# Two products on 64 partitions each for the image's row sums, and a spectrum kept in tiles of 128 partitions

## The chip, the cores and the metric

The kernel runs on one core of one Trainium2 chip. The metric is device time in microseconds (us) from launch to end; the number compared is the median of several executions.

## What is computed

A batch of 32 images of 56 x 56 pixels with 96 channels goes through two layers. Only the skeleton is kept here; `ln` is a normalization over the 96 channels.

```python
# layer 0: convolution
xz = einsum('bhwc,cd->bhwd', ln(x), w_in) + b_in        # 96 -> 2 * 192, first 192 kept
x  = x + silu(conv3x3(x1, conv_w) + conv_b)             # 192 -> 96
# layer 1: attention-like mixing by a Fourier transform over the 3136 tokens
h  = relu(bn1(einsum('bnc,hc->bnh', ln(t), w1)))        # 96 -> 192
X  = fft(h, axis=1, norm='ortho')
xr = relu(X.real * rd - X.imag * idg + rb)
xi = relu(X.imag * rd + X.real * idg + ib)
y  = ifft(xr + 1j * xi, axis=1, norm='ortho').real
t  = t + bn2(einsum('bnh,ch->bnc', y, w2))
# then a feed-forward layer 96 -> 384 -> 96 in 8-bit floats
t  = t + qlinear(relu(qlinear(ln(t), W1, b1)), W2, b2)
```

## The kernel before, in words

The work is a software pipeline over images. The class `Image` holds the state of one image, and `plan(b)` (L490) lists its steps: each `put(when, f, ...)` gives a step a due time in units of an eighth of an image. All steps of all images are sorted by due time (L556) and issued in that order. A scheduler of the language then places the instructions of each engine from that list; the order on TensorE is what it decides, and TensorE runs its products in that order. Pools with few buffers tie steps together: a step that takes a buffer waits until the buffer's earlier user has been read.

An image's 3136 tokens lie as 112 partitions times 28 columns, so that partition `2 * row + half` holds half of an image row. The steps that the change touches, with their lines:

- `fetch` (L335) loads columns of an image as `xl`; `take_in` (L343) computes their statistics with `stats` (L120) and scales them into `xa`.
- `image` (L144) multiplies `xa` with the constant `rows6_sb`, which forms the row sums that a fast convolution needs. One product of one column has 112 partitions of input, 97 columns of weights and 168 columns of output: 84 sums for each half of a row. The result `im` goes through ScalarE into `img`. Three columns share a PSUM tile of the pool `psq`, which has two buffers under the tag `q`; `conv` (L151, tiles `cv`) and `to_tokens` (L188, tiles `st`) use the same two.
- The Fourier transform has two stages with a trip through DRAM between them (`da`). The first is `product_a` (L200, tiles `ph`) and `transform_a` (L210, tiles `pa`). The second works on seven groups `g` of four frequency pairs each. `fetch_a` (L401) loads a group as `at`: 112 partitions, 4 pairs, 192 hidden channels. `forward` (L216, tiles `px`) multiplies one half `i` of the channels, 96 of them, of each pair with `fb_sb`; so the spectrum lies in tiles of 96 partitions, two for a group. Each tile then takes three ScalarE activations (L226 to L228), `parts` (L231: three VectorE operations and one of ScalarE) and `relus` (L243: two VectorE operations), which leave it in `gt`.
- `product_w2` (L248, tiles `pg`) multiplies by the output weights: for each pair two products of 96 partitions are added up. `inverse` (L259, tiles `pe`) transforms back, `store_back` (L429) stores the group to DRAM (`de`). When all seven groups are there, `fetch_y` (L432) reads `y`, and `back` (L438, `transform_out` L268, tiles `py`) does the last product.
- The feed-forward layer is `ffn_in` (L280, tiles `pf`) and `ffn_out` (L295, tiles `po`) in 8-bit floats.

All products but the last two are of 32-bit floats. Such a product runs as two passes, each a weight load and a matmul in the profile, so the profile counts two where the code has one; transposes (tiles `tp`, `st`) take one.

Due times of the second stage, which the change rewrites:

```python
for g in range(NS):
    put(max(FIRST + 7.4, g - 2.4), fetch_a, g)
    ...
    put(g + 1.15, second_w2, g)
    put(g + 1.35, second_back, g)
    put(g + 1.55, store_back, g)
```

Of the kernel before, what the change touches and what calls it, by code (L numbers as in the profile page):

```python
# [38 lines left out]
F32 = mybir.dt.float32  # L39
# [13 lines left out]
NS = NP // PG  # L53
H = 192
# [9 lines left out]
LN_W, LN_B, CONV_B, B_IN, BN1, BN2, RD, RB, NPAR = 0, 1, 2, 3, 5, 13, 17, 21, 25  # L64


def width(p):

    return 2 * N2 + (p < PG)


def first(p):

    return 2 * (2 * N2 * p + min(p, PG))
# [3 lines left out]
def hybrid_kernel(ctx: ExitStack, tc: tile.TileContext, x, par, w_in, conv_w, w1, w2, fw1, fb1, fw2, fb2, fa, fb, ib, ia, rows6, out):  # L78
# [8 lines left out]
    mhalf = const.tile([N1, N2], F32, name="mhalf")  # L87
# [7 lines left out]
    par_sb = const.tile([C, NPAR], F32, name="par_sb")  # L95
    convb = par_sb[:, CONV_B : CONV_B + 1]

    wv = const.tile([C + 1, WC, 3, C], F32, name="wv")
    rows6_sb = const.tile([N1, 2 * WC * WG], F32, name="rows6_sb")
    w1a = const.tile([C + 1, H], F32, name="w1a")  # L100
    w2a = const.tile([C, 2, C], F32, name="w2a")
# [6 lines left out]
    xas = [const.tile([N1, 8, C + 1], F32, name=f"xa{i}") for i in range(2)]  # L108
    img = const.tile([C + 1, 2, N2 + 2, WC, WG], F32, name="img")
    ys = [const.tile([113, G4, C], F32, name=f"y{i}") for i in range(4)]  # L110
    scal = const.tile([C, 3, 2], F32, name="scal")
# [8 lines left out]
    def stats(t, kind, b, i):  # L120


        n = t.shape[1]
        name = f"{kind}_{b}_{i}"
        st = stp.tile([N1, n, 3], F32, tag=f"st{kind}", name=f"st_{name}")
        for j in range(0, n, 2):
            nc.vector.bn_stats(  # L127
                st[:, j : j + 2].rearrange("p j s -> p (j s)"), t[:, j : j + 2, :C].rearrange("p j c -> p c j")
            )
        var = stp.tile([N1, n], F32, tag="var", name=f"var_{name}")  # L130
        nc.vector.tensor_scalar(var, st[:, :, 2], 1.0 / C, EPS, ALU.mult, ALU.add)  # L131
        rs = sums.tile([N1, n], F32, tag=f"rs{kind}", name=f"rs_{name}")
        nc.gpsimd.tensor_tensor(rs, var, mhalf[:, :n], ALU.pow)  # L133
        return st[:, :, 1], var, rs
# [9 lines left out]
    def image(xa, n, b, j0):  # L144

        ps = psq.tile([C + 1, n, 2, WC * WG], F32, tag="q", name=f"im_{b}_{j0}")
        for j in range(n):
            nc.tensor.matmul(ps[:, j], xa[:, j, :], rows6_sb, start=True, stop=True)  # L148
        nc.scalar.copy(img[:, :, j0 + 1 : j0 + 1 + n].rearrange("c h j k g -> c j h (k g)"), ps)
# [66 lines left out]
    def forward(at, b, g, i):  # L216

        w = width(g * PG)
        px = psum2.tile([C, PG, 2, w], F32, tag="c", name=f"px_{b}_{g}_{i}")
        for j in range(PG):  # L220
            p = g * PG + j
            nc.tensor.matmul(px[:, j], at[:, j, i * C : (i + 1) * C], fb_sb[:, first(p) : first(p + 1)], start=True, stop=True)  # L222
        idg, ibi = par_sb[:, RD + 2 + i : RD + 3 + i], par_sb[:, RB + 2 + i : RB + 3 + i]
        re, im = px[:, :, 0, :], px[:, :, 1, :]
        av = work.tile([C, 3, PG, w], F32, tag="av", name=f"av_{b}_{g}_{i}")
        nc.scalar.activation(av[:, 0], im, AF.Abs, scale=idg)  # L226
        nc.scalar.activation(av[:, 2], re, AF.Identity, scale=idg, bias=ibi)
        nc.scalar.activation(av[:, 1], re, AF.Relu, scale=scal[:, 0, i : i + 1], bias=scal[:, 1, i : i + 1])  # L228
        return px, av

    def parts(px, av, b, g, i):  # L231

        w = width(g * PG)
        rd, mrd = par_sb[:, RD + i : RD + i + 1], scal[:, 2, i : i + 1]
        re, im = px[:, :, 0, :], px[:, :, 1, :]
        sv = work.tile([C, 3, PG, w], F32, tag="sv", name=f"sv_{b}_{g}_{i}")
        nc.vector.scalar_tensor_tensor(sv[:, 0], re, rd, av[:, 0], ALU.mult, ALU.add)  # L237
        nc.vector.scalar_tensor_tensor(sv[:, 1], im, mrd, av[:, 2], ALU.mult, ALU.add)
        nc.scalar.activation(sv[:, 1], sv[:, 1], AF.Relu)
        nc.vector.scalar_tensor_tensor(sv[:, 2], im, rd, av[:, 2], ALU.mult, ALU.add)  # L240
        return sv

    def relus(sv, av, gt, i):  # L243
        rb = par_sb[:, RB + i : RB + i + 1]
        nc.vector.scalar_tensor_tensor(gt[:, i, :, 0, :], sv[:, 0], rb, av[:, 1], ALU.add, ALU.max)
        nc.vector.scalar_tensor_tensor(gt[:, i, :, 1, :], sv[:, 2], 0.0, sv[:, 1], ALU.max, ALU.subtract)  # L246

    def product_w2(gt, b, g):  # L248
        k = 2 * width(g * PG)
        pg = psum2.tile([k, PG, C], F32, tag="b", name=f"pg_{b}_{g}")  # L250
        for j in range(PG):
            for i in range(2):
                lhs = gt[:, i, j].rearrange("c r k -> c (r k)")
                nc.tensor.matmul(pg[:, j, :], lhs, w2a[:, i, :], start=(i == 0), stop=(i == 1))  # L254
        gw = work.tile([k, PG, C], F32, tag="gw", name=f"gw_{b}_{g}")
        nc.scalar.copy(gw, pg)
        return gw

    def inverse(gw, b, g):  # L259

        pe = psum2.tile([112, PG, C], F32, tag="b", name=f"pe_{b}_{g}")
        for j in range(PG):
            nc.tensor.matmul(pe[:, j, :], ib_sb[: gw.shape[0], g * PG + j, :], gw[:, j, :], start=True, stop=True)
        es = work.tile([112, PG, C], F32, tag="es", name=f"es_{b}_{g}")
        nc.scalar.copy(es, pe)
        return es
# [68 lines left out]
    def fetch(im, i):  # L335
# [4 lines left out]
        im.xl[i] = xnp.tile([N1, j1 - j0, C], F32, tag=tag, bufs=bufs, name=f"xl_{im.b}_{i}")  # L340
        nc.sync.dma_start(im.xl[i], im.tokens[:, j0:j1, :])

    def take_in(im, i):  # L343
# [5 lines left out]
        nc.vector.tensor_tensor(im.xa[i][:, :n, :C], xl, rs.unsqueeze(2).to_broadcast([N1, n, C]), ALU.mult)  # L349
# [57 lines left out]
    def second(im, g, i):  # L407
        im.held["px", g, i] = forward(im.at[g], im.b, g, i)
        if i == 1:
            im.at.pop(g)  # L410

    def second_parts(im, g, i):
        px, av = im.held.pop(("px", g, i))
        im.held["sv", g, i] = parts(px, av, im.b, g, i), av

    def second_relus(im, g, i):
        if i == 0:
            im.gt[g] = work.tile([C, 2, PG, 2, width(g * PG)], F32, tag="gt", name=f"gt_{im.b}_{g}")
        relus(*im.held.pop(("sv", g, i)), im.gt[g], i)

    def second_w2(im, g):
        im.gw[g] = product_w2(im.gt.pop(g), im.b, g)

    def second_back(im, g):
        if g == 0:
            im.de = dram.tile([NP, 112, C], F32, tag="de", name=f"de_{im.b}")
        im.held["es", g] = inverse(im.gw.pop(g), im.b, g)

    def store_back(im, g):  # L429
        nc.sync.dma_start(im.de[g * PG : (g + 1) * PG].rearrange("p m c -> m p c"), im.held.pop(("es", g)))  # L430
# [44 lines left out]
    def ffn_end(im, g):  # L475
        o = im.held["o", g] = w3.tile([N1, G4, C], F32, tag="o", name=f"o_{im.b}_{g}")
# [13 lines left out]
    def plan(b):  # L490
# [5 lines left out]
        for i, (j0, j1) in enumerate(LN_CHUNKS):  # L496
# [3 lines left out]
            ats = (-0.95, -0.7) if last else (0.2, 0.5, 0.85) if i == 2 else (0.25, 1.0, 1.5)  # L500
            put(at + ats[0] - (2.5 if b else 12), fetch, i)
            put(at + ats[0] - 1.15, take_in, i)
            for part, j in enumerate(range(0, j1 - j0, 3)):
                put(at + ats[part], make_image, i, j, min(3, j1 - j0 - j))
# [34 lines left out]
        for g in range(NS):  # L539
            put(max(FIRST + 7.4, g - 2.4), fetch_a, g)  # L540
            for i in range(2):
                at = g + 0.55 * i
                put(at, second, g, i)
                put(at + 0.22, second_parts, g, i)
                put(at + 0.42, second_relus, g, i)
            put(g + 1.15, second_w2, g)
            put(g + 1.35, second_back, g)
            put(g + 1.55, store_back, g)
# [21 lines left out]
    with tc.tile_pool(name="setup", bufs=1) as sp, tc.tile_pool(  # L570
# [3 lines left out]
        nc.sync.dma_start(par_sb, par)  # L574
        win = sp.tile([C, H], F32, name="win")
# [63 lines left out]
        w2s = sp.tile([C, H], F32, name="w2s")  # L639
        nc.sync.dma_start(w2s, w2)  # L640
        nc.vector.tensor_scalar(w2s, w2s, s2, None, ALU.mult)
        for g in range(2):
            ps = spp.tile([128, 512], F32, tag="ps", name=f"ps_w2{g}")
            nc.tensor.transpose(ps[:C, :C], w2s[:, g * C : (g + 1) * C], ident[:C, :C])
            nc.vector.tensor_copy(w2a[:, g, :], ps[:C, :C])
# [9 lines left out]
        nc.vector.tensor_scalar(scal[:, 0, :], par_sb[:, RD : RD + 2], 2.0, None, ALU.mult)  # L655
        nc.vector.tensor_scalar(scal[:, 1, :], par_sb[:, RB : RB + 2], 2.0, None, ALU.mult)
        nc.vector.tensor_scalar(scal[:, 2, :], par_sb[:, RD : RD + 2], -1.0, None, ALU.mult)
# [40 lines left out]
def dft_tables():  # L698
# [57 lines left out]
    rows6 = np.zeros((HW, 2, 2, WC, WG))  # L756
    for g in range(WG):
        for i in range(6):
            r = 4 * g + i - 1
            if 0 <= r < HW:  # L760
                for h in range(2):
                    rows6[r, h, h, :, g] = sums[:, i]
    tables = fa.reshape(N1, 112), fb.reshape(112, -1), ib.reshape(114, NP, 112), ia, rows6.reshape(N1, -1)
    return [np.ascontiguousarray(a, np.float32) for a in tables]

# [45 lines left out]
```

## Time and profile before

| what | value |
|---|---|
| median of 3 runs | 3287.43 us (3282.76 to 3293.95) |
| profiled execution, its own time | 3285.59 us |
| its span, first to last instruction | 3283.7 us |
| granted TensorE clock over the span | 0.989 |
| VectorE (DVE) busy | 2711.9 us, 83% |
| ScalarE (ACT) busy | 2319.2 us, 71% |
| GpSimd (POOL) busy | 586.2 us, 18% |
| DMA | 355.61 MB, mean 108 GB/s |

Busy time is the union of an engine's instructions in time. In the lists of groups each row is a line, an engine, an operation, the tile written, the tiles read, the shapes, the count, then busy us and mean ns of one. For TensorE the shapes read: partitions x weight columns of the weights, then partitions x columns of the moving operand. PE is TensorE's matmul, PEld its weight load. Matmuls are pipelined: one begins before the one ahead has ended, so what a matmul costs is read from start to start and not from its duration.

### The profile page before, as it was taken

To read this page: it belongs to the slowest core of one execution; us is meant where nothing else is said; L and a number is where in the kernel's file an instruction comes from. 1 tells how busy PE (TensorE), PEld (TensorE's weight loads), DVE (VectorE), ACT (ScalarE), POOL (GpSimd) and SP (SyncE) were. 2 spreads that over 40 slices of the span, in tenths; PEclk is the share of its full clock that TensorE was granted. 3 is DMA by queue.
4 is the path that set the end of the run, shared out by engine and by line. 5 is a ranking of instruction groups with operands and counts; after the bars stand their busy time and mean duration, and the time that the engine had idled before them with its cause. 6 is when DMAs were issued, how large, how long until landed. Compare 5 with 4: busy or idle time off the path is not lost. (4 is left out here: it accounts for less than half of the span.)

```text
span 3283.7 us, 69648 instructions
## 1 busy us (share of the span) xinstructions
PE 3201.2 (97%) x24597; PEld 2821.3 (86%) x24597; DVE 2711.9 (83%) x8306; ACT 2319.2 (71%) x5616; POOL 586.2 (18%) x397
## 2 busy tenths in 40 slices
PE   6999999999999999999999999999999999999987
PEld 5888888888888888888888888888888888888875
DVE  5568888888888888888888888888888888887887
ACT  2567777777777777777777776777777777777676
POOL 2111112111112111112111112111112111111111
PEclk9999999999999999999999999999999999999997
DMA  4343344433344433344433344433344333443331
GB/s 109 102 110 104 96 114 121 118 105 108 92 121 123 118 102 106 98 119 121 117 106 100 104 121 117 118 97 103 107 121 123 106 108 94 116 121 104 98 108 55
DMA packets 330839, 355.61 MB, mean 108 GB/s; under 512 B 125577, under 2 KB 283673, under 8 KB 330265
## 3 DMA queue, kind: packets, MB, share of 16 engines
q1 hardware_dynamic: 328482, 348.99, 38.5%
q8 instruction: 195, 3.19, 0.4%
q10 hardware_dynamic: 2008, 2.17, 0.2%
q14 instruction: 154, 1.25, 0.1%
HBM read 196.92 MB, written 154.14 MB: 107 GB/s over the span
## 5 line engine op out<-in xcount | busy, mean ns | idle before, releaser
L159 PE MATMUL cv<-img,wv 97*96 97x224 f32 (+1 forms) x4608 | 863.8, 330 | 6.2 <-DVE wv L607 5.4
L159 PEld LDWEIGHTS cv<-img,wv 97*96 97x96 f32 x4608 | 675.1, 163 | 88.1 <-issue 7.1
L133 POOL TENSOR_TENSOR rs_c<-var_c,mhalf 112x8 f32<-112x8 f32 (+1 forms) x128 | 194.1, 1517 | 1900.5 <-DVE var_a L131 994.0
L222 PEld LDWEIGHTS px<-fb_sb,at 112*96 112x96 f32 x3584 | 399.7, 164 | 87.7 <-issue 30.6
L222 PE MATMUL px<-fb_sb,at 112*96 112x112 f32 (+1 forms) x3584 | 429.8, 261 | 20.6 <-DMA at<-da 17.4
L254 PEld LDWEIGHTS pg<-w2a,gt 96*112 96x112 f32 (+1 forms) x3584 | 394.2, 179 | 33.4 <-DVE gt L246 2.9
L254 PE MATMUL pg<-w2a,gt 96*112 96x96 f32 (+1 forms) x3584 | 403.9, 262 | 1.4 <-DVE gt L246 0.6
L226 ACT ACTIVATE av<-px,par_sb 96x224 f32<-96x224 f32 (+1 forms) x448 | 200.1, 447 | 267.8 <-PE px L222 263.4
L284 ACT CAST h<-pf 128x448 f16<-128x448 f32 x672 | 362.5, 539 | 25.2 <-PE pf L282 22.2
L204 PE MATMUL ph<-w1a,n2t 97*112 97x192 f32 x1792 | 369.0, 328 | 1.5 <-ACT n2t L197 1.2
L213 PE MATMUL pa<-h,fa_sb 112*112 112x384 f32 x896 | 366.3, 491 | 0.1
L207 ACT ACTIVATE h<-ph,rs_b 112x192 f32<-112x192 f32 x896 | 330.3, 426 | 29.3 <-PE ph L204 27.9
L148 PE MATMUL im<-rows_sb,xa 112*97 112x168 f32 x1792 | 324.0, 308 | 11.3 <-DVE xa L349 9.6
L133 POOL TENSOR_TENSOR rs_b<-var_b,mhalf 112x8 f32<-112x8 f32 (+1 forms) x128 | 191.7, 1498 | 748.1 <-DVE var_b L131 423.9
L204 PEld LDWEIGHTS ph<-w1a,n2t 97*112 97x112 f32 x1792 | 286.8, 177 | 39.5 <-ACT n2t L197 1.8
L292 DVE TENSOR_SCALAR h<-h,b1q 128x448 f16<-128x448 f16 x658 | 214.2, 326 | 112.0 <-ACT h L284 110.7
L459 DVE TENSOR_SCALAR xn<-t,st_c,rs_c 112x96 f32<-112x96 f32 x896 | 240.0, 320 | 75.4 <-POOL rs_c L133 75.3
L148 PEld LDWEIGHTS im<-rows_sb,xa 112*97 112x97 f32 x1792 | 263.9, 165 | 35.0 <-issue 10.3
L214 ACT COPY u<-pa 112x384 f32<-112x384 f32 x448 | 216.5, 483 | 101.3 <-PE pa L213 97.4
L293 DVE CAST hq<-h 128x448 fp8e5<-128x448 f16 x672 | 257.2, 383 | 12.7 <-ACT h L290 5.9
L237 DVE SCALAR_TENSOR_TENSOR sv<-px,par_sb,av 96x224 f32<-96x224 f32 (+1 forms) x448 | 197.4, 441 | 70.9 <-ACT av L228 66.1
L282 PE MATMUL pf<-n3t,w1q 96*128 96x448 fp8e5 x672 | 242.2, 360 | 8.8 <-ACT h L284 7.6
(110 smaller groups left out, 6022.9 us busy)
## 6 DMA issues: line engine op xcount, KB each, us to landing
da<-u SPq DMA_DIRECT2D x224, 336.0 KB, 3.2
at<-da SPq DMA_DIRECT2D x224, 336.0 KB, 3.8
de<-es SPq DMA_DIRECT2D x224, 168.0 KB, 2.3
y<-de SPq DMA_DIRECT2D x224, 168.0 KB, 2.8
out<-o SPq DMA_DIRECT2D x224, 168.0 KB, 2.2
xl<-in_x SPq DMA_DIRECT2D x96, 336.0 KB, 3.9
x<-in_x SPq DMA_DIRECT2D x96, 336.0 KB, 3.2
xl<-in_x SPq DMA_DIRECT2D x32, 168.0 KB, 2.3
```

Source lines behind the costliest of these rows:

```text
L133: nc.gpsimd.tensor_tensor(rs, var, mhalf[:, :n], ALU.pow)
L148: nc.tensor.matmul(ps[:, j], xa[:, j, :], rows6_sb, start=True, stop=True)
L159: nc.tensor.matmul(ps[:, at], wv[:, k, dx, :], cols, start=(dx == 0), stop=(dx == 2))
L204: nc.tensor.matmul(ph[:, j, :], n2t[:, 2 * j2 + j, :], w1a, start=True, stop=True)
L207: nc.scalar.activation(h[:, j], ph[:, j], AF.Relu, scale=rs[:, 2 * j2 + j : 2 * j2 + j + 1])
L213: nc.tensor.matmul(pa, fa_sb, h, start=True, stop=True)
L222: nc.tensor.matmul(px[:, j], at[:, j, i * C : (i + 1) * C], fb_sb[:, first(p) : first(p + 1)], start=True, stop=True)
L254: nc.tensor.matmul(pg[:, j, :], lhs, w2a[:, i, :], start=(i == 0), stop=(i == 1))
L282: nc.tensor.matmul(pf, w1q[:, k * 128 : (k + 1) * 128], n3t, start=True, stop=True)
L284: nc.scalar.copy(h1, pf)
L293: nc.vector.tensor_copy(hq[:, k, :], h2, saturate=False)
L459: nc.vector.tensor_scalar(xc[:, j], im.t[i][:, at, :C], mu[:, at : at + 1], rs[:, at : at + 1], ALU.subtract, ALU.mult)
```

## The change

The image's row sums. The host lays a second copy of the input, `xh`, in which the left halves of the 56 rows are on partitions 0 to 55 and the right halves on partitions 64 to 119; the rest is zeros. One column now takes two products, one for each block of 64 partitions, with 84 columns of output each, into two PSUM tiles at once. A step does 4 columns in place of 3, and its result goes through two ScalarE copies.

The spectrum. The seven groups become four units of 8, 8, 8 and 4 frequency pairs. In a unit of 8 there are three tiles of 128 partitions: two hold channels 0 to 127 of four pairs each, the third holds channels 128 to 191 of all eight, four pairs on partitions 0 to 63 and four on 64 to 127. The third is made by products of 64 weight columns that write one half of the partitions or the other. In `product_w2` one product of 192 columns, whose weights `w2y` are zero where the halves cross, serves the third tile for two pairs, and one of 96 columns for each pair adds channels 0 to 127. The results of four pairs are stored by two DMAs in place of one. `width` is 57 for eight pairs in place of four. The pool of the output tile `o` has two buffers in place of three.

```diff
 def image(xa, n, b, j0):
-        ps = psq.tile([C + 1, n, 2, WC * WG], F32, tag="q", name=f"im_{b}_{j0}")
+        ps = [psq.tile([C + 1, n, WC * WG], F32, tag="q", name=f"im_{b}_{j0}_{h}") for h in range(2)]
         for j in range(n):
-            nc.tensor.matmul(ps[:, j], xa[:, j, :], rows6_sb, start=True, stop=True)
-        nc.scalar.copy(img[:, :, j0 + 1 : j0 + 1 + n].rearrange("c h j k g -> c j h (k g)"), ps)
+            for h in range(2):
+                rows = slice(64 * h, 64 * h + 64)
+                nc.tensor.matmul(ps[h][:, j], xa[rows, j, :], rows6_sb[rows], start=True, stop=True)
+        for h in range(2):
+            nc.scalar.copy(img[:, h, j0 + 1 : j0 + 1 + n].rearrange("c j k g -> c j (k g)"), ps[h])
...
-    def forward(at, b, g, i):
-        px = psum2.tile([C, PG, 2, w], F32, tag="c", name=f"px_{b}_{g}_{i}")
-        for j in range(PG):
-            p = g * PG + j
-            nc.tensor.matmul(px[:, j], at[:, j, i * C : (i + 1) * C], fb_sb[:, first(p) : first(p + 1)], start=True, stop=True)
+    def forward(ats, b, m, u):
+        p0, p1 = UNITS[m]
+        n = PG if u < 2 else (p1 - p0) // 2
+        px = psum2.tile([128, n, 2, w], F32, tag="c", name=f"px_{b}_{m}_{u}")
+        for j in range(n):
+            for half in range(1 if u < 2 else 2):
+                p = p0 + u * PG + j if u < 2 else p0 + half * n + j
+                rows = slice(0, 128) if u < 2 else slice(64 * half, 64 * half + 64)
+                lhs = ats[p // PG][:, p % PG, :128] if u < 2 else ats[p // PG][:, p % PG, 128:]
+                nc.tensor.matmul(px[rows, j], lhs, fb_sb[:, first(p) : first(p + 1)], start=True, stop=True)
...
-        for j in range(PG):
-            for i in range(2):
-                lhs = gt[:, i, j].rearrange("c r k -> c (r k)")
-                nc.tensor.matmul(pg[:, j, :], lhs, w2a[:, i, :], start=(i == 0), stop=(i == 1))
-        nc.scalar.copy(gw, pg)
+        for j in range(2):
+            lhs = gt[:, 2, j0 + j].rearrange("c r k -> c (r k)")
+            nc.tensor.matmul(pg[:, :, j, :], lhs, w2y, start=True, stop=False, skip_group_check=True)
+            for half in range(2):
+                p = four(m, j0)[half][j] - UNITS[m][0]
+                lhs = gt[:, p // PG, p % PG].rearrange("c r k -> c (r k)")
+                nc.tensor.matmul(pg[:, half, j, :], lhs, w2x, start=False, stop=True, skip_group_check=True)
+        nc.scalar.copy(gw.rearrange("k h j c -> k (h j c)"), pg.rearrange("k h j c -> k (h j c)"))
...
-    def store_back(im, g):
-        nc.sync.dma_start(im.de[g * PG : (g + 1) * PG].rearrange("p m c -> m p c"), im.held.pop(("es", g)))
+    def store_back(im, m, j0):
+        p0, p1 = UNITS[m]
+        es = im.held.pop(("es", m, j0))
+        rows = im.de[p0:p1].rearrange("(h j) m c -> m h j c", h=2)
+        for half in range(2):
+            nc.sync.dma_start(rows[:, half, j0 : j0 + 2], es[:, half])
...
-        o = im.held["o", g] = w3.tile([N1, G4, C], F32, tag="o", name=f"o_{im.b}_{g}")
+        o = im.held["o", g] = work.tile([N1, G4, C], F32, tag="o", name=f"o_{im.b}_{g}")
...
-            ats = (-0.95, -0.7) if last else (0.2, 0.5, 0.85) if i == 2 else (0.25, 1.0, 1.5)
+            ats = (-0.95,) if last else (0.2, 0.85) if i == 2 else (0.25, 1.25)
...
-            for part, j in enumerate(range(0, j1 - j0, 3)):
-                put(at + ats[part], make_image, i, j, min(3, j1 - j0 - j))
+            for part, j in enumerate(range(0, j1 - j0, 4)):
+                put(at + ats[part], make_image, i, j, 4)
...
-            put(max(FIRST + 7.4, g - 2.4), fetch_a, g)
-            for i in range(2):
-                at = g + 0.55 * i
-                put(at, second, g, i)
-                put(at + 0.22, second_parts, g, i)
-                put(at + 0.42, second_relus, g, i)
-            put(g + 1.15, second_w2, g)
-            put(g + 1.35, second_back, g)
-            put(g + 1.55, store_back, g)
+            put(max(FIRST + 7.4, g - (1.4 if g % 2 else 2.2)), fetch_a, g)
+        for m, (p0, p1) in enumerate(UNITS):
+            both = p1 - p0 > PG
+            for at, u in ((0, 0), (0.62, 1), (1.25, 2)) if both else ((0, 0), (0.62, 2)):
+                at += 2 * m
+                put(at, second, m, u)
+                put(at + 0.22, second_parts, m, u)
+                put(at + 0.42, second_relus, m, u)
+            for j0 in range(0, (p1 - p0) // 2, 2):
+                at = 2 * m + (2 if both else 1.3) + 0.2 * j0
+                put(at, second_w2, m, j0)
+                put(at + 0.2, second_back, m, j0)
+                put(at + 0.4, store_back, m, j0)
```

## The prediction

> **What bounds the kernel now.** I read the busy shares first, then the table of stretches, then the waits of TensorE, then its order of time.
>
> ```profile
> PE 3201.2 (97%) x24597; PEld 2821.3 (86%) x24597; DVE 2711.9 (83%) x8306; ACT 2319.2 (71%) x5616; POOL 586.2 (18%) x397
> ```
> ```profile
> 330.00:2930.00 2600.00, 2581.34 (x20119) 2291.98 (x20118) 2210.46 (x6773) 1886.60 (x4593) 476.50 (x315) 1.00 0.40 111
> 2930.00:3284.00 354.00, 321.10 (x2420) 266.87 (x2418) 286.88 (x889) 247.44 (x592) 51.25 (x32) 0.92 0.33 91
> ```
> ```profile
> PE px L222 <- DMA at<-da: 12.7, 17, 1.3
> PE py L271 <- DMA y<-de: 3.8, 5, 1.6
> ```
>
> In 2600 us of steady state TensorE is busy for 2581, at full clock, and its two longest waits come to 16.5 us; VectorE is busy for 85% and ScalarE for 73%. So TensorE's stream sets the time. Busy time alone would not prove it, since matmuls overlap, so I priced every product from start to start, on runs of equal products (timeline of TensorE, and of its loads in the setup):
>
> ```profile
> 1620.78 0.93 PE L222 MATMUL px<-fb_sb,at 112*96 112x112 f32 x8
> ...
> 1630.23 1.72 PE L254 MATMUL pg<-w2a,gt 96*112 96x96 f32 x16
> ...
> 1633.22 0.73 PE L148 MATMUL im<-rows_sb,xa 112*97 112x168 f32 x4
> ```
> ```profile
> 28.96 0.76 PEld L597 LDWEIGHTS ps_we<-cw,wt 96*97 96x97 f32 x8 [1.05 <-DVE weff L598]
> ```
>
> The second number is the length of the run. Less the last matmul (260, 261, 308 ns by the groups), divided by count less one: px 670/7 = 96 ns, pg 1459/15 = 97 (98 over all runs), im 422/3 = 141 (142). The last line is a run whose weights have 97 columns and whose operand has only 96: (760 - 165)/7 = 85 ns, 86 over all. So a pass costs the larger of its columns x 0.833 + 2.3 ns (112: 96; 168: 142; 192: 162) and its weight columns x 0.833 + 4.7 (97: 86; 112: 98; 114: 100; carried on, 128: 112). pg is bound by its load, px and im by columns. These prices times the counts give 3134 us for all of TensorE's work, of the execution's 3285.6; 125 of the remaining 152 us I find as gaps, 38 in the 2600 us above, most of the rest in the first 200 us and the last 280. Whatever changes TensorE's passes moves the time one to one.
>
> [...] In the program before, [...]ps_o with one weight column[...]. It shows no drain:
>
> ```profile
> 42.01 0.25 PE L644 MATMUL ps_w<-ident,w2s 96*96 96x96 f32 x1
> ...
> 42.09 0.24 PE L647 MATMUL ps_o<-ident,o 96*1 96x96 f32 x1
> ...
> 42.18 1.11 PE L159 MATMUL cv<-img,wv 97*96 97x224 f32 x5
> ```
>
> Starts are 80 to 90 ns apart, the price of 96 columns (82)[...]. For column tiles I therefore take 0. For row tiles the trace shows nothing.
>
> **The change part by part.** Counts are passes, two for a product: 32 images x 28 columns or pairs.
>
> *Spectrum, forward (px).* Before: 3584 x 96 = 344 us. After: 1792 with 128 weight columns, 112 ns by the load: 201. And 1792 with 64 weight columns and 112 of operand. In the changed program's order they stand as asked: the two halves alternate (718 of 896 products follow another of their kind). If the two overlap, a run of 16 passes takes 9 turns of 97 ns, 98 us in all; if their loads (64 x 0.833 + 4.7 = 58) come one after the other, 104. I take 110, as some runs are broken up. If they do not overlap, 1792 x 97 = 174. Change: -33, at the other end +31.
>
> *Output weights (pg).* Before 3584 x 98 = 351. After: for two pairs one pass of 192 columns (162) and two of 96 (98): 896 x 162 + 1792 x 98 = 321. Change: -30. That its output has a step is a row no trace shows; 96 floats lie together, and I price it at 0.
>
> *Row sums (im).* Before 1792 x 142 = 254. The code alternates halves, but in the changed program's order the scheduler has put the four products of half 0 together and then those of half 1, usually with other products between: only 127 of 1343 neighbours alternate. [...] So 3584 passes, 84 columns (72 ns) but 97 weight columns (86 ns): 308. Change: +54. Below that: if loads were hidden, 3584 x 72 = 258 (+4).
>
> *Change of mode.* The order has 869 changes between row tiles and full products and 28 between row and column tiles, 897 in all. Bounds for one: 0, as ps_o shows, and a full drain, a matmul's 260 ns less its 97 of stream, 163 ns: 146 us. I take 20 ns, 18 us[...].
>
> *The way back through DRAM.* Before, the last `pe` of an image leads to the first `py` like this:
>
> ```profile
> 1599.73 0.94 PE L263 MATMUL pe<-gw,ib_sb 112*112 112x96 f32 x8
> 1600.70 0.48 ACT L265 COPY es<-pe 112x384 f32<-112x384 f32 x1
> 1601.87 0.38 SPq L430 DMA_DIRECT2D de<-es  x1
> 1603.86 0.32 SPq L481 DMA_DIRECT2D out<-o  x1
> 1606.76 2.15 SPq L436 DMA_DIRECT2D y<-de  x4
> 1609.10 0.27 PEld L271 LDWEIGHTS py<-y,ia_sb 113*112 113x112 f32 x2 [0.26 <-issue]
> ```
>
> 8.5 us pass from the end of `pe` to `py`, and the products between, priced as above, come to 8.5: exactly covered. Now the last store stands 0.15 later in the due times, is two DMAs (another 0.3 us of SP's issue, with the reads of `y` queued behind it), and the products between come to 7.1 us in two images of three and 9.2 in the third. A shortfall of up to 1.4 us in 21 images is 30 us, 40 with the second issue; part of the chain is SP's queue (0.7 us ahead of the store) and may give, so I take 12, from 0. SP itself has room: 224 further issues of 0.3 us are 70 us, beside other work.
>
> *ScalarE, VectorE, PSUM.* Per image 14 tiles of 96 partitions become 10 of 128 and one of half the columns. A tile costs ScalarE 448 + 529 + 532 + 403 = 1.9 us and VectorE 4 x 437 + 379 = 2.1; about 6.3 and 6.9 us less per image, 200 and 220 in all. Image copies go from 11 to 14 per image (7 x 580 + 3 x 434 + 328 = 5.7 us against 14 x 434 = 6.1): +12. None of this is TensorE's, so it counts only where TensorE waits: in the last 280 us (60 us of gaps) I take -5, at most -20. Against it, `im` now holds both `psq` buffers at once, 33 users per image in place of 30, with `cv` and `st` waiting behind; I price that at 0 because the order has other products between, and put up to 20 into the upper end. `o` with two buffers, `at` fetched in turns, the 14% more bytes of `xl` (DMA is 40% busy): 0, covered by 12 us of due time each; uncovered, a late `xl` or `at` costs what it costs now, 1.3 us at a time.
>
> *Sum.* 3285.6 - 33 - 30 + 54 + 18 + 12 - 5 = 3302. The profiled execution is 1.8 us under the median of the runs, which I leave.
>
> **The rivals.**
> - *Faster: cheaper half-loads.* If a load into 64 rows slips entirely under the product ahead, row sums cost 72 ns a pass and come out at +4; with free mode changes and a covered way back, 3285.6 - 33 - 30 + 4 + 0 + 7 = 3234. It decides below 79 ns for a pass, where `im` falls under 283 us and the sum under 3277. Against it: the 86 ns of ps_we. For it: no row-tiled load is in the trace. At the far end, halves that overlap though grouped, 43 ns a pass, 3130.
> - *Pairs do not overlap.* px +31 in place of -33: 3366. For it: no overlap of 32-bit products in the trace, and each has two passes on one tile, in order. Against: the program alternates them.
> - *Row modes drain.* 897 x 163 = 146 in place of 18: 3430; half of it, 3360. [...]against, ps_o.
> - *The change does not do what it says* for the row sums: by the order it does not; that is in my forecast.
>
> **How the numbers follow.** Forecast (pairs overlap, row sums bound by loads, small switches) 0.40, between 3270 and 3335. Faster rival 0.17, no overlap 0.18, drain 0.25. Low end: the faster rival at 3234 with part of it left out, 3250. High end: drain whole, 3430; drain with no overlap (3494) is left out. What measurement can tell here is about 0.3%, 10 us. Faster than 3277: 0.17 + 0.05 of the forecast's lower part = 0.22. Within 10 us: 0.17. Slower: the rest of the forecast and both slow rivals, 0.61.
>
> **What would show it.** `im` start to start at 86 ns (72 or 43: the faster rival); the tiled px starting every 50 to 60 ns on average (97: no overlap); px of 128 weight columns at 112; the first product after `im` starting late by over 100 ns (drain); `py` waiting for `y` by about 0.5 us an image. VectorE near 2490 and ScalarE near 2130 us. Wrong altogether if the gaps of TensorE in steady state, 38 us now, exceed 80 without a change of mode ahead of them.

## The result, and the profile after

| | median | range | ratio to before, 95% interval |
|---|---|---|---|
| before, beside it | 3288.9 us (4 runs) | 3282.76 to 3293.95 | |
| after | 3400.91 us (4 runs) | 3398.54 to 3403.79 | 1.0335 [1.0318, 1.0352] |

The change makes the kernel 3.4% slower. The profiled execution of the changed kernel took 3402.66 us, its span is 3400.9 us, the granted clock over it 0.990. That is 117.2 us more span than before, and the time is about 100 us above the forecast of 3302. The share of each engine, from the page:

```profile
PE 3339.0 (98%) x25493; PEld 2805.4 (82%) x25493; DVE 2545.3 (75%) x7829; ACT 2233.0 (66%) x5328; POOL 584.5 (17%) x397
```

VectorE gave back 167 us and ScalarE 86, as the larger tiles should; TensorE has 16 us *less* of loads, and yet 138 us more of busy matmul. The steady stretch again, and the last 371 us (in each line the stretch, its length, busy time and instructions of PE, PEld, DVE, ACT and POOL, then the granted clock, the share of DMA and its GB/s):

```profile
330.00:2930.00 2600.00, 2593.92 (x20030) 2186.95 (x20029) 1993.66 (x6115) 1748.45 (x4183) 455.18 (x302) 1.00 0.38 108
3030.00:3401.00 371.00, 342.56 (x2619) 279.87 (x2616) 286.87 (x902) 253.31 (x602) 55.03 (x35) 0.94 0.34 97
```

The granted clock is 1.00 again in the steady stretch, so a lower clock does not explain it. TensorE is busy for 2594 us of 2600, more than before (2581): by busy time it does better, by the result it does worse. Its waits for the two trips through DRAM did not grow either. The prediction showed them for the steady stretch alone; here and in what follows a line of waits is of a whole execution and gives the microseconds in total, the times and the longest. First the kernel before, then the changed one:

```profile
PE px L222 <- DMA at<-da: 17.4, 20, 2.5
...
PE py L271 <- DMA y<-de: 8.2, 8, 2.5
```
```profile
PE px L237 <- DMA at<-da: 7.3, 7, 2.8
...
PE py L298 <- DMA y<-de: 5.2, 8, 1.3
```

So the time is inside TensorE's stream, between products that wait for nothing. The order of time (start, length, engine, line, tiles, count) of TensorE's matmuls and loads shows where, in a stretch in which each kind of product comes once:

```profile
1604.93 0.96 PEld L290 LDWEIGHTS pe<-gw,ib_sb 114*112 114x112 f32 x8
1605.12 0.93 PE L290 MATMUL pe<-gw,ib_sb 114*112 114x96 f32 x8
1605.98 1.17 PEld L156 LDWEIGHTS im<-rows_sb,xa 64*97 64x97 f32 x16
1605.99 1.33 PE L156 MATMUL im<-rows_sb,xa 64*97 64x84 f32 x16
1607.24 0.60 PEld L213 LDWEIGHTS ph<-w1a,n2t 97*112 97x112 f32 x4
1607.24 0.90 PE L213 MATMUL ph<-w1a,n2t 97*112 97x192 f32 x4
1607.82 0.13 PEld L146 LDWEIGHTS tp_n<-ident,xn 112*96 112x96 f32 x1
1607.98 0.26 PE L146 MATMUL tp_n<-ident,xn 112*96 112x112 f32 x1
1608.82 0.41 PE L237 MATMUL px<-fb_sb,at 112*64 112x112 f32 x4
1609.46 0.58 PEld L237 LDWEIGHTS px<-fb_sb,at 112*64 112x64 f32 x12 [0.20 <-issue]
1609.46 0.80 PE L237 MATMUL px<-fb_sb,at 112*64 112x112 f32 x12
1610.18 0.17 PEld L146 LDWEIGHTS tp_n<-ident,xn 112*96 112x96 f32 x2
```

Eight `pe` passes at their price of 98 ns from 1605.12 end their turn at 1605.90; the first tiled `im` starts at 1605.99, 0.09 us late. And its weight load starts with it, at 1605.98, while `pe`'s first load was made 0.19 us ahead of its matmul. The same on the way out: `ph` starts with its load, both at 1607.24, and four `ph` of 162 ns from 1607.24 end their turn at 1607.89, but the next product comes at 1607.98, 0.09 late: the first load of `ph` was made in the open, that is, when its own matmul was due and not ahead of it. That next product, a full-array `tp_n` after a full-array `ph`, has its own load 0.16 ahead (1607.82 against 1607.98). The tiled `px` run of 12 passes takes (0.80 - 0.26) / 11 = 49 ns a pass where 96 would be one after the other: the pairs overlap.

Priced over the whole trace as the prediction did it (start to start, less the price of the pass), TensorE's stream splits like this:

| TensorE, us start to start | before | after | difference |
|---|---|---|---|
| passes at their prices | 3131 | 3180 | +49 (im +52, px +28, pg -30) |
| overlap of the `px` pairs | 0 | -72 | -72 |
| overlap of `im` halves, where a run's two halves touch | 0 | -10.5 | -10.5 |
| last product ahead of a change of mode, late by | 0 | 129 | +129 |
| first product after a change, late by | 0 | 69 | +69 |
| gaps elsewhere | 138 | 91.5 | -47 |

The sum is +118, against 117.2 of span. A change of mode is a step between the full array, tiles of 64 rows and tiles of 64 columns in the order in which the trace has the products: 1225 of them, 198 us, 162 ns each. Some 16 of these 198 us are not the change itself: at 33 of the changes the next product is over 110 ns late, for the most part because it also waits for the setup's weights or for `at`. Without them a change costs about 149 ns, and the gaps fell by some 31 us and not 47. The gain of the overlap, of `pg` and of the gaps is real, and smaller.

### The profile page after: what moved, and what is told of

It reads as the page before. It is cut to its first block, busy times and chain, and to the rows that moved or that the text cites. A ratio compares the mean times of both kernels' runs of the same rounds, so it can differ in the third digit from the quotient of the medians.

```text
span 3400.9 us, 70310 instructions
## 1 busy us (share of the span) xinstructions
PE 3339.0 (98%) x25493; PEld 2805.4 (82%) x25493; DVE 2545.3 (75%) x7829; ACT 2233.0 (66%) x5328; POOL 584.5 (17%) x397
## 4 chain that ended last, share of the span: by engine, by line
PE 93%; DMA 4%; DVE 2%; ACT 1%; issue 0%; SPq 0%; ACTq 0%; DVEq 0%
PE cv L168 22%; PE im L156 10%; PE px L237 9%; PE ph L213 9%; PE pa L222 9%; PE tp_n L146 5%; PE pe L290 5%; PE pg L280 5%; PE pg L276 5%; PE py L298 4%; PE po L326 4%; PE pf L309 4%; PE st L200 2%; DMA de<-es 1%; DMA at<-da 1%; DMA da<-u 1%
## 5 line engine op out<-in xcount | busy, mean ns | idle before, releaser
L168 PE MATMUL cv<-img,wv 97*96 97x224 f32 (+1 forms) x4608 | 898.4, 332 | 0.9 <-DVE sd L180 0.9
L156 PEld LDWEIGHTS im<-rows_sb,xa 64*97 64x97 f32 x3584 | 326.9, 166 | 98.1 <-issue 36.8
L156 PE MATMUL im<-rows_sb,xa 64*97 64x84 f32 x3584 | 396.8, 261 | 9.1 <-DVE xa L376 8.6
L237 PEld LDWEIGHTS px<-fb_sb,at 112*64 112x64 f32 (+1 forms) x3584 | 328.0, 165 | 90.5 <-issue 54.9
L237 PE MATMUL px<-fb_sb,at 112*64 112x112 f32 (+3 forms) x3584 | 390.5, 275 | 8.7 <-DMA at<-da 7.3
L213 PE MATMUL ph<-w1a,n2t 97*112 97x192 f32 x1792 | 382.6, 332 | 0.0
L253 DVE SCALAR_TENSOR_TENSOR sv<-px,spar_sb,av 128x224 f32<-128x224 f32 (+2 forms) x352 | 153.1, 435 | 151.4 <-ACT av L244 150.1
L158 ACT COPY img<-im 97x336 f32<-97x336 f32 x448 | 193.8, 444 | 99.9 <-PE im L156 96.3
L280 PE MATMUL pg<-w2x,gt 128*112 128x96 f32 (+1 forms) x1792 | 253.2, 259 | 0.0
L280 PEld LDWEIGHTS pg<-w2x,gt 128*112 128x112 f32 (+1 forms) x1792 | 245.3, 178 | 5.5
```

The costliest lines, as they stand in the source:

```text
L156: nc.tensor.matmul(ps[h][:, j], xa[rows, j, :], rows6_sb[rows], start=True, stop=True)
L168: nc.tensor.matmul(ps[:, at], wv[:, k, dx, :], cols, start=(dx == 0), stop=(dx == 2))
L213: nc.tensor.matmul(ph[:, j, :], n2t[:, 2 * j2 + j, :], w1a, start=True, stop=True)
L237: nc.tensor.matmul(px[rows, j], lhs, fb_sb[:, first(p) : first(p + 1)], start=True, stop=True)
L280: nc.tensor.matmul(pg[:, half, j, :], lhs, w2x, start=False, stop=True, skip_group_check=True)
```

## The experiments

The theory after the result: at a change of mode the next product starts about 93 ns late, and the load of that product isn't made ahead of it, another 65 to 90 ns, both as in the changed kernel's trace. The rivals: the row products cost more by themselves (loads of 64 rows that do not hide), or the spectrum costs it. The first four kernels ran on one chip together, where the kernel before gave 3289.8 us; with the next four it gave 3291.5 and with the last two 3290.4, and each ratio is to the kernel before beside it.

### One half of the change alone: `rows_only`

The kernel before with the new row sums (second copy of the input, two products a column, steps of four), and its spectrum untouched:

```diff
-            nc.tensor.matmul(ps[:, j], xa[:, j, :], rows6_sb, start=True, stop=True)
+            for h in range(2):
+                rows = slice(64 * h, 64 * h + 64)
+                nc.tensor.matmul(ps[h][:, j], xa[rows, j, :], rows6_sb[rows], start=True, stop=True)
...
```

> The kernel before with the row-sum half of the change alone; its order has 935 changes of mode. Theory (each change of mode costs about 165 ns: some 93 ns until the next product starts and 65 to 90 ns because that product's load could not be made ahead): row sums +52 us by their loads, -21 where halves alternate (252 of 1324 neighbours), 935 x 165 = +154, less gaps -20: about 3450 us, 3420 to 3470. Rival (changes of mode are cheap and the loss of the whole change comes from the spectrum's longer units or the shared PSUM buffers): about 3317 us.

Measured: 3445.9 us, ratio 1.0468 [1.0442, 1.0494], 156 us slower than before and inside the expected range. Its profiled execution was 11 us under that median. Split as above, against the profiled execution of before: passes +51.6, 935 changes 154 us, overlap -15, gaps 138 to 98. Within a run of eight row passes, as in the line below, the starts are 151, 86, 86, 86, 86, 86, 86 and 176 ns apart: inside, a pass costs exactly the load of 97 columns that was forecast (86, from `ps_we` with 96 rows), so a row pass costs no more than was forecast. The first is 65 late and the last 90, and the product ahead of the run has already lost 93. The wait for `at` did not grow (17.4 us before):

```profile
1618.91 0.91 PE L151 MATMUL im<-rows_sb,xa 64*97 64x84 f32 x8
```
```profile
PE px L226 <- DMA at<-da: 10.4, 13, 2.4
```

### The other half alone: `spectrum_only`

The changed kernel with the row sums as they were before:

```diff
-            for h in range(2):
-                rows = slice(64 * h, 64 * h + 64)
-                nc.tensor.matmul(ps[h][:, j], xa[rows, j, :], rows6_sb[rows], start=True, stop=True)
+            nc.tensor.matmul(ps[:, j], xa[:, j, :], rows6_sb, start=True, stop=True)
...
```

> The changed kernel with the row sums as they were; 328 changes of mode, all between column tiles and full products. Theory: forward products -52, output weights -30, 328 x 165 = +54, gaps of TensorE -30: about 3228 us, 3205 to 3250, faster than before. Rival (the units' longer way and the double stores hold TensorE up, and the loss is theirs): 3290 us or more.

Measured: 3282.81 us, ratio 0.9978 [0.9965, 0.9991]: 7 us faster than before, where 62 were expected. Passes -2, pairs -75, 328 changes 40 us: that alone is -37. The rest is in the gaps, which went from 138 to 169 us, those of the steady stretch from 39.5 to 78.8. Waits of TensorE, and the steady stretch:

```profile
PE px L233 <- DMA at<-da: 36.3, 32, 2.8
PE py L294 <- DMA y<-de: 13.1, 19, 1.7
```
```profile
330.00:2930.00 2600.00, 2555.68 (x19348) 2210.77 (x19347) 2054.20 (x6365) 1790.33 (x4264) 464.43 (x314) 1.00 0.39 111
```

`px` waits 32 times for `at`, once for each image, 36.3 us where it was 17.4 in the kernel before, and `py` 19 times for `y`, 13.1 us where it was 8.2. Both are the trips through DRAM. All these waits of `px` stand at an image's first unit (114 columns of operand), whose `fetch_a` has the same due time before and after, so they don't come from the later fetches of the other groups. A stream that is shorter by a microsecond an image reaches the trips sooner, but that this is the cause is not shown: `probe_full` below has a stream 200 us longer than the kernel before and waits at the same place for 38.0 us. In the changed kernel the two waits are small (7.3 and 5.2 us). The gaps are also why the halves do not add up: +156 and -7 make 149, and together they cost 112; the gaps differ by 38 us, the changes of mode hardly (154 + 40 against 198).

### The change of mode by itself: `probe_full`, `probe_modes`, `probe_why`

Three kernels add a small product at four places of the kernel before: 16 columns of operand after `pa`, `pe` and `py`, and one more transpose after `st`, each into an unused piece of the PSUM tile. In `probe_full` they use the full array, in the other two a tile. The line at `pa` in the three of them, in this order:

```diff
+        nc.tensor.matmul(bank[:112, 448:464], fa_sb[:112, :112], h[:112, 0, :16], start=True, stop=True)
+        nc.tensor.matmul(bank[:112, 448:464], fa_sb[:64, :112], h[:64, 0, :16], start=True, stop=True)
+        nc.tensor.matmul(bank[:112, 448:464], fa_sb[:32, :112], h[:32, 0, :16], start=True, stop=True)
```

| place | `probe_full` | `probe_modes` | `probe_why` |
|---|---|---|---|
| after `pa` | 112 rows, 112 columns | 64 rows | 32 rows |
| after `pe` | 112 weight columns | 64 weight columns | 64 weight columns |
| after `py` | 112 weight columns | 32 weight columns | 1 weight column |
| after `st` (transpose) | 96 weight columns | 1 weight column | 64 weight columns |

> The kernel before with one small extra product, whose result is not used, after each pa, pe, py and each group of four transposes st, all as full products (control). 448 x 2 passes of 98 ns at pa, 224 x 2 at pe and at py, 224 transposes of 82: +194 us of TensorE, gaps -30: about 3450 us. No product starts late.

> The same extra products, but in tiles: 64 rows at pa, 64 weight columns at pe, 32 at py, one weight column of a transpose at st. Loads are shorter (pe 58 ns, py 31), so the work is 146 us. Theory: 2240 changes at 165 ns, 369 us: about 3770 us; in the trace both the first product in the mode and the first after it start some 90 ns late. If a 32-column tile is free of it[...], 896 changes cost nothing and it is about 3620. Rival (changes cheap): about 3400 us.

> probe_modes with other shapes of the extra product: 32 rows at pa, 64 weight columns at pe as before, one weight column of an ordinary product at py, 64 weight columns of a transpose at st. It asks why the one product of the setup showed nothing. If transposes are exempt, st costs no more than its 82 ns and py shows some 90 ns on each side; if one weight column is exempt, it is the other way round. 32 rows should cost what 64 rows did, about 280 ns over the full product for the way in and out.

Measured, one run each: 3489.78, 3626.85 and 3614.72 us. `probe_full` came out 40 us above its expectation; it waits longer for `at` than the kernel before (17.4 us), although its stream is the longer one:

```profile
PE px L226 <- DMA at<-da: 38.0, 28, 4.2
```

`probe_modes` missed by 143 us. That it lies near 3620, the time that stood for a free tile of 32 columns, is chance: the table shows that this tile pays and that the transposes are what pays nothing. By place, as the median of what one small product adds to the stream, in ns:

| place | full | `probe_modes` | `probe_why` |
|---|---|---|---|
| after `pa` | 183 | 466 | 464 |
| after `pe` | 213 | 403 | 403 |
| after `py` | 181 | 334 | 301 |
| after `st` | 87 | 87 | 87 |

By their counts (448 at `pa`, 224 at each other place) the differences of `probe_modes` to `probe_full` come to 204 us. The times differ by 137: the wait for `at` fell to 4.4 us, and other gaps with it.

In these probes the price does not depend on the size of the tile: 32 rows cost what 64 do (464 and 466 ns), and one weight column costs 301 where 32 cost 334, its two loads taking 0.09 us in the order of time where those of 32 took 0.14. But it does depend on the operation: the transposes, whether with one weight column or with 64, cost the 87 of a full one and pay nothing. The order of time in `probe_modes`, at `pa` and at `st`:

```profile
1809.64 0.81 PE L216 MATMUL pa<-h,fa_sb 112*112 112x384 f32 x2
1810.38 0.27 PEld L217 LDWEIGHTS pa<-h,fa_sb 64*112 64x112 f32 x2 [0.56 <-issue]
1810.38 0.36 PE L217 MATMUL pa<-h,fa_sb 64*112 64x16 f32 x2
...
1813.16 0.49 PE L192 MATMUL st<-ident,s 96*112 96x96 f32 x4
1813.41 0.08 PEld L193 LDWEIGHTS st<-ident,s 96*1 96x1 f32 x1
1813.49 0.25 PE L193 MATMUL st<-ident,s 96*1 96x96 f32 x1
```

Two `pa` of 322 ns from 1809.64 end their turn at 1810.28; the small product starts at 1810.38, 0.10 late, its load with it. Four `st` of 82 from 1813.16 end at 1813.49, and the narrow transpose starts right then, its load 0.08 ahead. In `probe_why` the product of one weight column and the transpose of 64 stand the other way round from what their sizes would suggest:

```profile
1801.09 0.81 PE L278 MATMUL py<-y,ia_sb 113*112 113x384 f32 x2
1801.83 0.09 PEld L279 LDWEIGHTS py<-y,ia_sb 112*1 112x1 f32 x2 [0.56 <-issue]
1801.83 0.20 PE L279 MATMUL py<-y,ia_sb 112*1 112x16 f32 x2
...
1812.71 0.50 PE L192 MATMUL st<-ident,s 96*112 96x96 f32 x4
1812.96 0.11 PEld L193 LDWEIGHTS st<-ident,s 96*64 96x64 f32 x1
1813.04 0.25 PE L193 MATMUL st<-ident,s 96*64 96x96 f32 x1
```

1801.09 + 0.64 is 1801.73, and the product comes at 1801.83: it pays. 1812.71 + 0.33 is 1813.04: the transpose does not. The product `ps_o`, on which the prediction had based its price of a column tile, is a transpose. Whether a narrow transpose is placed in a tile at all, no run shows.

### The halves in turn: `rows_turn`

The scheduler had put the four products of one half together. An edge that fixes only the order, with no semaphore, keeps them in turn:

```diff
-                nc.tensor.matmul(ps[h][:, j], xa[rows, j, :], rows6_sb[rows], start=True, stop=True)
+                mm = nc.tensor.matmul(ps[h][:, j], xa[rows, j, :], rows6_sb[rows], start=True, stop=True)
+                if j + h:
+                    tc.add_manual_dep(mm.ins, last.ins.name, ORDER, reason="halves in turn")
+                last = mm
```

> The changed kernel with one thing different: an order edge from each row-sum product to the next, so that the two halves stand in turn (1346 of the neighbours, 127 before); changes of mode stay at 1224. Theory (the row sums lose because the scheduler put the halves in groups, besides the changes of mode): a run of 2n passes takes n + 1 turns of 86 ns, (1792 - 446) x 86 = 116 us less, of which 10 are had already: -105, given back in part as gaps: about 3310 us, 3285 to 3330. Rival (halves do not overlap even in turn, or loads of two row tiles come one after the other): about 3400.

Measured: 3385.3 us, ratio 1.0289 [1.0269, 1.031], 16 us faster than the changed kernel and not 90. The order of time, the waits, and the steady stretch:

```profile
1814.06 0.92 PE L157 MATMUL im<-rows_sb,xa 64*97 64x84 f32 x16
```
```profile
PE px L241 <- DMA at<-da: 30.8, 27, 3.7
```
```profile
330.00:2930.00 2600.00, 2556.99 (x20181) 2137.82 (x20180) 1998.23 (x6170) 1720.51 (x4211) 472.14 (x304) 0.99 0.39 109
```

The row tiles do overlap: 16 passes take 0.92 us where they took 1.33, in pairs 7 ns apart and a pair every 85 to 86 ns. Over the trace `im` fell from 379 to 294 us start to start. But of these 85 us 45 came back as gaps (91.5 to 136.5), above all as the same wait for `at`, and some 20 more at column tiles and at products next to a change of mode. The granted clock was lower too, 0.984 over the span where the changed kernel had 0.990. The expectation missed; it was right that halves in turn overlap, and left out who is late next. The changes of mode stayed: the edge fixes the order among the row products, and the scheduler still put others between them. Most runs are broken in two, 181 of 2 passes and 144 of 14, and only 30 are whole. A whole run of 16, four columns, takes 852 ns from its first start to the next product (nine of the 17 in the steady stretch; the other eight take 953), 93 more ahead of it and 91 to 100 after it, about 1040 ns; without tiles it is eight full passes at 142, 1136 ns. So even whole runs in turn would save at best some 96 ns each, about 21 us on 224 of them; a broken one pays a second way in and out and loses more than that.

### The spectrum with its steps earlier: `spectrum_early`

`spectrum_only` waits for DRAM, so the steps of the other stages get due times that stand earlier or later by 0.12 to 0.2 of an eighth of an image:

```diff
-    CONV, FIRST, BACK, FFN = -12.3, -8, 8.38, 10.85
+    CONV, FIRST, BACK, FFN = -12.5, -8.2, 8.5, 10.97
```

> The spectrum half alone, with the stages ahead of the spectrum 0.2 earlier in the due times and those behind it 0.12 later. Theory: what spectrum_only lost against its sum are TensorE's waits for at from DRAM (36 us) and for y (13 us), because a faster TensorE reaches them sooner; with more time between they fall to about 10: about 3245 us, 3230 to 3262. Rival (the waits move elsewhere, since other buffers are held longer): 3275 or more.

Measured: 3252.93 us, ratio 0.9894 [0.9873, 0.9915]: inside the expected range, and faster than the kernel before and the changed one. Its waits, and the steady stretch:

```profile
PE cv L164 <- ACT img L154: 13.1, 20, 1.5
...
PE px L233 <- DMA at<-da: 7.2, 7, 2.0
PE py L294 <- DMA y<-de: 6.9, 11, 1.2
```
```profile
330.00:2930.00 2600.00, 2579.86 (x19505) 2230.36 (x19504) 2091.81 (x6431) 1801.04 (x4306) 522.23 (x317) 1.00 0.40 111
```

The wait for `at` fell from 36.3 to 7.2 us and that for `y` from 13.1 to 6.9, while a new one of 13.1 came at `cv`. Gaps of the steady stretch went from 79 to 53.

### Fewer changes of mode: `spectrum_prio`

`spectrum_early` with the products of `forward` at high priority, which cuts the changes from 320 to 256 in the program's order:

```diff
+        with tc.high_priority():
-        for j in range(n):
+            for j in range(n):
...
```

> spectrum_early with the forward products of the spectrum at a higher priority, so that the scheduler puts nothing between the products of one tile: 256 changes of mode in place of 320. Theory: 64 changes fewer at 165 ns is -11 us: about 3235 us against 3245 for spectrum_early. Rival (a product placed early makes TensorE wait for at): no better, or worse.

Measured: 3326.48 us, ratio 1.0108 [1.0088, 1.0127]. The rival was right. The waits of TensorE:

```profile
PE px L234 <- DMA at<-da: 44.0, 31, 2.6
PE ph L209 <- DVE t L475: 38.6, 27, 2.4
```

At some 150 ns each, 64 changes less are worth about 10 us (an estimate from the changed kernel's trace); products pulled to the front make TensorE stand at them until their inputs are there, and the gaps of the steady stretch became 134 us.

### Whose gain is it: `before_early`, `rows_turn_early`

The same line of due times in the kernel before, and in `rows_turn`.

> Control: the kernel before with the due times of spectrum_early and nothing else. Theory (the gain of spectrum_early is the spectrum in tiles of 128 partitions; the due times only make room for it): the waits for at and y in the kernel before come to 17 us in the steady state, so about 3278 us, 3265 to 3292. Rival (the due times alone are the gain): about 3253.

> rows_turn with the due times of spectrum_early; by its order 1086 changes of mode in place of 1224. Theory (what rows_turn gave back was TensorE's wait for at, 31 us, and the rest of its loss is changes of mode): 3385 less 25 for the wait and 138 x 165 = 23: about 3340 us, 3325 to 3365, still slower than before. Rival (the gaps belong to the row tiles themselves, which hold both PSUM buffers): 3375 or more.

Measured: `before_early` 3319.71 us, ratio 1.0085 [1.0066, 1.0104]; `rows_turn_early` 3397.31 us, ratio 1.0312 [1.0287, 1.0338]. Both expectations missed: both kernels became slower. Waits of `before_early`, then of `rows_turn_early`:

```profile
PE pa L213 <- ACT h L207: 26.3, 34, 1.2
...
PE cv L159 <- DVE t L375: 8.2, 14, 1.4
```
```profile
PE px L241 <- DMA at<-da: 49.1, 31, 2.6
```
```profile
330.00:2930.00 2600.00, 2552.97 (x20040) 2131.75 (x20040) 2001.34 (x6119) 1712.52 (x4183) 503.51 (x303) 0.98 0.38 108
```

In `before_early` the wait for `at` fell from 17.4 to 5.2 us, but one of 26.3 came at `pa`, and the gaps of the steady stretch went from 39.5 to 69. So the 39 us of `spectrum_early` are not a gain that the due times bring to any version: the kernel before loses 29 us by them. In `rows_turn_early` the very wait that the shift should have cured grew from 30.8 to 49.1. The last line shows a second loss, a granted clock of 0.98 in the steady stretch, where the changed kernel had 1.00; over the span it is 0.975 against 0.990. In the changed kernel's trace a `cv` pass of 224 columns starts 189 ns after the one ahead where the granted clock is 1.00, and 373 ns after it where it is 0.5. So part of this kernel's loss is slower passes and no waits; how much, and what brought the clock down, is not shown. A shift of a due time moves the scheduler's whole order; which part of it sets the wait for `at` is not settled by these runs.

## Why the prediction was wrong in size, and where it was right

The time lay in the range of 3250 to 3430, 99 us above the predicted value and outside the 3270 to 3335 of the forecast itself. The range held it because the rival "row modes drain" had been given room in it, not because the forecast's working was right. The sum had seven terms:

| step | predicted, us | measured, us |
|---|---|---|
| spectrum forward | -33 | -44 (passes +28, overlap -72) |
| output weights | -30 | -30 |
| row sums | +54 | +41 (passes +52, overlap at the seam of the halves -10.5) |
| change of mode, rows | +18 | +156 (some 15 of it waits at the same places) |
| change of mode, columns | 0 | +42 |
| way through DRAM, relief at the end | +12 - 5 | -47 |

**Change of mode: the step that failed.** "I take 20 ns, 18 us." The counts were right, 897 changes with row tiles in it; the size was near its upper bound: 156 us are 174 ns each, 157 without the waits that fall on the same places. The estimate of a full drain, a matmul's 260 ns less 97 of stream, gave 163. That this is nearly the right size is luck, for its working had only half of what the trace shows: a next product 90 to 94 ns late, and a load in the open on top, 65 to 91 ns. What TensorE does in the 90 ns is not shown. By the letter of the sign to look for, a first product after `im` late by over 100 ns, these 90 would even have counted against a drain. The rival "row modes drain" had the direction and the price, with 0.25 of the chance.

**"For column tiles I therefore take 0."** This failed in kind. `ps_o` was one instruction, and a transpose; `probe_modes` and `probe_why` show that a narrow transpose pays nothing where a product of one weight column pays 92 ns on the way in alone. The trace of before contained no ordinary product of 64 rows or 64 weight columns, so it could tell nothing of the price; the changed kernel's has some 149 ns on the mean of 1225 changes. That narrow transposes paid nothing does not speak against it, since no run shows that they change the mode.

**Spectrum forward** came out better than its term, since the column pairs run as the prediction's lower value had it: 98 us in all by the working, 100 in the changed kernel (172 at price less 72). The sign to look for, 50 to 60 ns on average, is met with 49 in the run shown; `px` of 128 weight columns stands at 112 as worked out. "Pairs do not overlap" fell: in the changed kernel's trace the two of a pair start 7 ns apart, and the next pair 89 after.

**Row sums.** 86 ns start to start inside a run, as forecast, in `rows_only` too: the faster rival, a load that hides, fell. That a load of 64 rows costs what one of 96 does was the author's estimate until then. Passes of one half did not overlap, as the 86 ns show; at the seam, where two groups of different halves touch, 10.5 us of overlap came in all. What `rows_turn` adds is that halves in turn cost one load price for two loads, a pair per 85 to 86 ns: two loads in the time of one. The faster rival's 3234 has a slip that changes nothing: it calls the way back covered and yet keeps its +7; with -5 in its place it is 3222.

**The way through DRAM.** `py` waits 5.2 us and not 0.5 an image, so nothing was paid. That doesn't show that there is cover: `spectrum_only` pays 36.3 us at `at` and 13.1 at `y`. The prediction took gaps as nearly fixed beside the passes; in these kernels they are not. They fell by 47 us (some 31 when the waits at changes of mode are counted in), grew by 31 in `spectrum_only` and fell by 40 in `rows_only`. These three would fit a slower stream that gives each trip more time, but `probe_full` does not: its stream is 200 us longer than before, and its wait for `at` grew from 17.4 to 38.0 us.

**VectorE and ScalarE** came to 2545 and 2233 us, 55 and 103 above what was forecast; no effect of that on the time is to be seen, with TensorE busy for 2594 of 2600 us.

**What would make it wrong altogether**, gaps in the steady stretch over 80 us without a change of mode, did not come: 22 us.

Open is what in the scheduler's order makes the wait for `at` come and go, and with it whether row halves in turn together with the spectrum could be brought below `spectrum_early`.

## What to carry to other kernels

Before tiles of the array are used, count in the program's own order how often ordinary products change between full array, row tiles and column tiles, and set what the changed kernel's trace showed, about 149 ns, against each; a run in the mode has to save more than its way in and out. Four columns of row sums saved at best 96 ns of 1136, and only in an unbroken run in turn. The best version here, `spectrum_early` at 0.9894 of the time before, keeps the half of the change with few changes and long runs in the mode, drops the other, and has due times under which TensorE waits less. Which due times those are had to be tried: the same shift made two other versions slower. And evidence for a price must come from the same kind of instruction: here the transposes paid 0 ns on the way in, and a product of one weight column 92.

## What the runs showed of the hardware

- At a change of mode between ordinary 32-bit products the next one started 90 to 94 ns late (medians of the changed kernel), and that one's weight load was not made ahead, 65 ns for 97 columns in 64 rows and 75 to 91 for full 32-bit products; transposes and 8-bit products that came first on the way out took 6 (`pf`), 34 (`po`), 49 (`st`) and 78 ns (`tp_n`) more than the 193, 52, 82 and 96 ns they take start to start without a change, also medians of the changed kernel. The way in was 92 to 94 ns in the probes for 64 and for 32 rows and for 64, 32 and one weight column; after their short products the way out was 76 to 90. Between row and column tiles it was 90 to 93.
- Narrow transposes (one or 64 weight columns) after full ones cost no change: 0 ns late in and 87 ns in all, what a full one costs. Whether they lie in a tile is open.
- Two tiles in turn, 32-bit: column tiles of 64 with 112 columns of operand, starts 7 and 89 ns; row tiles of 64 with 97 weight columns, 7 and 78, though each would take 86 by its load alone.
- A TensorE that is busy for 99.8% of the steady stretch (2593.92 of 2600) can hold some 180 us of changes of mode over the span: the shown durations of the matmuls cover them. Only start to start shows them.
